# Layer 0's statistics by batch-norm instructions, a replanned order with late loads, and the last mask on TensorE, in a two-layer graph kernel

## The chip, the cores and the metric

The kernel runs on one core of a Trainium2 chip. The metric is the device time of one execution in microseconds (us), as a median of a few executions; lower is better. A core has TensorE (PE, matrix products), VectorE (DVE), ScalarE (ACT), GpSimd (POOL) and SyncE (SP, whose queue issues nearly all DMA transfers here: all but 6 of the 901 issues that the profile of the kernel before lists).

## The reference, cut to what matters

The input x is 128 batches of 128 nodes by 512 features. Layer 0 has the same adjacency for both weights, so its inner max collapses to one number per row.

```python
A = einsum('od,bdn->bon', adj, x)                 # "conv"
out0 = max_n(relu(A + b))  -> one number r per row
x = layernorm(x + r)                              # layer 0
qkv = x @ w_qkv;  8 heads
attn = softmax(where(mask == 0, -inf, q k^T * scale))
o = (attn v) @ w_proj + b_proj
x = layernorm(x + o + layernorm(o) * gamma + beta)  # layer 1
```

Adding r to a whole row does not change the row's variance and moves its mean by r. So the statistics of x + r follow from those of x, which are known as soon as x is loaded. The change uses this.

## The kernel before

Batches go in groups of four. For each group TensorE does twelve "dense" products (q, k, v; each product in three split parts), four scores, four attention products, four output projections, and the conv of a group two ahead. The kernel gives each engine its instructions in the order of one plan, a list sorted by a planned time. The planned times come from a table O of offsets from the TensorE step to which an operation belongs. An offset thus decides what stands ahead of what on each engine, and nothing else.

```python
def add_0(b):                 # ScalarE: x + r in place, with the row sum
    nc.scalar.activation(xs[b], xs[b], AF.Identity, bias=rms[g][:, i:i+1], accum_out=mv0s[g][:, i, 0:1])
def stats_0(b):               # ScalarE: sum of squares about the mean
    squares(xs[b], mv0s[g][:, i, :])
...                           # rstd_0, shift_0: five small GpSimd operations
def norm_0(b):                # ScalarE: normalize in place
    nc.scalar.activation(xs[b], xs[b], AF.Identity, bias=nm, scale=rstd)
def x_halves(b):              # ScalarE copies x into two planes of half words; SyncE stores them ("rowsx")
    planes = work.tile([P, 2, D], U16, tag="xplanes", bufs=1)
    nc.scalar.copy(planes, ...)
    nc.sync.dma_start(rows["x", b], planes)
def crossbar_x(b):            # SyncE: transposing load; xT takes a buffer of the same four as load_x
    pts[b] = xpool.tile([P, KC, P], FP, tag="xt")
    nc.sync.dma_start_transpose(pts[b]..., rows.pop(("x", b))...)
def halves(b): ...            # the same for the attention weights: ScalarE copy of 1.8 us, "planes", then "rows"
def crossbar_T(b): ...        # transposing load eT, read by the attention product
def split_d(key, gpsimd): ... # residue part x_d = x_h - x_l..., on VectorE or GpSimd by a flag 'd'
...
O = {'softmax': {'halves': [1.11, 11.24, 0.39, 2.34], 'weights': [10.99, 14.73, 21.85, 34.94], ...},
     'stats_0': [-7.16, -8.5, 6.68, -15.05], ... 'two': {'d': [1, 0, 1, 0, 0, 1, 0, 1], ...}}
```

Of the kernel before, what the change touches and what calls it, by code (L numbers as in the profile page):

```python
# [26 lines left out]
def tile_adj_resnorm_d2(  # L27
# [198 lines left out]

    def norm_0(b, vector=False):
        rstd, nm = norms.pop((b, 0))
        if vector:
            nc.vector.tensor_scalar(xs[b], xs[b], rstd, nm, op0=ALU.mult, op1=ALU.add)  # L230
            return
        nc.scalar.activation(xs[b], xs[b], AF.Identity, bias=nm, scale=rstd)  # L232
# [117 lines left out]
    def scores(b):  # L350
# [4 lines left out]
        pscs[b] = psc = ps_2.tile([P, 2, HP, P], FP, tag="ps2", name=f"psc_{b}")  # L355
        for hp in range(HP):
            for s in range(2):
# [3 lines left out]
                    start=True, stop=True,  # L361
                )

    def masked(b):
        if b < B - 1:
            e = work.tile([P, H, P], FP, tag="e", bufs=3, name=f"e_{b}")
        else:

            e = work.tile([P, 2, H * P], U16, tag="planes", bufs=1, name=f"e_{b}")
            e = e.rearrange("p s m -> p (s m)").bitcast(FP).rearrange("p (h m) -> p h m", h=H)  # L370
        nc.vector.scalar_tensor_tensor(  # L371
# [3 lines left out]
        es[b] = e  # L375

    def row_max(b):
        nmax = small.tile([P, H], FP, tag="nmax", name=f"nmax_{b}")
        nc.vector.tensor_reduce(nmax, es[b], AX.X, ALU.max, negate=True)  # L379
        es[b] = es[b], nmax  # L380

    def exps(b):
        e, nmax = es[b]
        sums = small.tile([P, H], FP, tag="sums", name=f"sums_{b}")
        for j in range(H):
            nc.scalar.activation(  # L386
                e[:, j, :], e[:, j, :], AF.Exp, bias=nmax[:, j : j + 1],
                accum_out=sums[:, j : j + 1],
            )
# [81 lines left out]
    def residual_o(b):  # L471
        engine = nc.gpsimd if b < B - G else nc.vector
# [35 lines left out]
    def norm_2(b):  # L508
# [9 lines left out]
    O = {'add_0': [-28.01, -2.67, 12.08, -40.74],  # L518
 'conv_max': [4.55, 4.72, 6.29, 4.66],
 'dense_order': [('dense', 4), ('dense', 5), ('conv', 3), ('conv', 2), ('dense', 6), ('dense', 8),  # L520
                 ('dense', 7), ('dense', 11), ('dense', 10), ('dense', 9)],
 'final': {'norm_1': [5.56, 10.5, 14.34, 13.61],
           'norm_2': [12.82, 25.73, 75.6, 26.29],
           'residual': [-18.87, -9.5, -3.43, -8.74],
           'residual_o': [5.36, 6.15, 8.98, 4.31],
           'residual_x': [-41.8, -51.69, -15.49, -25.59],
           'stats_1': [5.17, 9.89, 7.71, 8.6],
           'stats_2': [12.28, 13.13, 19.78, 20.53]},
 'last': {'norm_1': [9.58, 9.14, 7.67, 8.6],
          'norm_2': [13.12, 22.67, 13.86, 10.82],  # L530
          'residual': [-2.72, -10.61, 6.62, -30.79],
          'residual_o': [3.24, 7.11, 7.11, 5.39],
          'residual_x': [-30.28, -1.34, -16.65, -32.32],
          'stats_1': [5.84, 4.73, 7.43, 4.32],
          'stats_2': [9.71, 14.36, 12.44, 9.12]},
 'load': [0.06, -0.01, -14.55, -3.61],
 'main': [2.3, -0.65, -0.19, 0.11, 5.34, 0.19, 4.21, -1.68, -1.36, -0.44, 0.62, -1.65],
 'norm_0': [16.54, 23.0, -1.62, 2.96],
 'norm_1': {'norm_1': [15.62, 20.63, 12.47, 19.45],
            'norm_2': [19.7, 33.16, 22.1, 38.56],  # L540
            'residual': [-0.58, -15.25, 2.03, 5.96],
            'residual_o': [5.96, 9.31, 4.86, 18.97],
            'residual_x': [19.5, -11.28, 9.99, -11.76],
            'stats_1': [10.06, 13.22, 5.06, 7.83],
            'stats_2': [17.31, 22.7, 14.78, 24.32]},
 'o_d': [15.21, 7.81, 2.7, 7.93],
 'o_high': [3.47, -4.38, -3.96, 9.85],
 'o_hl': [0.41, 5.8, 1.75, 8.23],
# [3 lines left out]
 'po_main': [0.7, -1.26, 2.4, -0.02],  # L552
 'po_rest': [0.12, 0.1, 1.9, 0.12],
 'pro': {'add': [-13.57, -12.84, -10.58, -8.9],
         'conv_max': [-14.9, -13.17, -12.81, -10.03],
         'copy': [-10.01, -7.16],
         'd': [-6.26, -20.85, -4.47, -9.88],
         'gamma': [42.69],
         'high': [-19.62, -3.45, -16.17, -13.31],
         'keep': [-1.39, 0.62],  # L560
         'load': [-4.65, -6.62, 1.94, 0.39],
         'norm': [-10.64, -8.84, -7.55, -2.23],
         'relu': [-13.82, -12.91, -10.66, -9.37],
         'rstd': [-13.4, -9.99, -8.25, -3.85],
         'split': [-7.87, -6.72, -3.41, -3.99],
         'stat': [-13.43, -12.09, -8.81, -4.38],
         'w': [-7.75, -6.02, -3.34, 1.69, 4.45, 6.04, 7.57, 11.57, 13.9, 13.27, 22.03, 16.92, 41.13,
               46.85, 57.05, 54.2],
         'wrest': [-7.26, 6.82, -0.99, 3.59, -9.44, 9.43, 6.9, 4.63, 7.79, 15.59, 14.21, 1.4, 21.84,
                   31.66, 38.37, 46.51]},  # L570
 'pro_order': [('conv', 0), ('conv', 1), ('conv', 2), ('conv', 3), ('x', 0), ('x', 1), ('v', 0),
               ('x', 2), ('v', 1), ('x', 3)],
 'relu_0': [6.8, -8.71, 1.47, -7.29],
 'rest': [6.51, 1.71, 1.45, 0.9, 11.28, 4.35, 11.73, -0.79, 1.66, -0.35, 0.99, 4.88],
 'rstd_0': [16.44, -5.55, 4.82, -18.77],
 'softmax': {'cross': [-12.79, -9.61, -18.95, -6.28],
             'exps': [10.86, 9.05, 42.17, 22.92],
             'halves': [1.11, 11.24, 0.39, 2.34],
             'masked': [0.34, 3.01, 1.47, 17.35],
             'row_max': [16.52, 12.06, 18.4, 20.81],  # L580
             'weights': [10.99, 14.73, 21.85, 34.94]},
 'stats_0': [-7.16, -8.5, 6.68, -15.05],
# [254 lines left out]
```

## Time and profile before

| quantity | before |
|---|---|
| time, median of 3 (range) | 1981.43 us (1975.82 to 1982.25) |
| profiled span, mean granted clock | 1978.3 us, 0.990 |
| busy: PE, DVE, ACT, POOL | 1860.2, 1617.9, 1625.2, 1328.5 us |
| start, middle, end | 91.2, 1784.1, 102.9 us |

Start, middle and end are cut at the first instruction of the q/k product 6 of group 1 and of group 31. Inside the middle I cut each group at two more places. **d9** is the end of ScalarE's copy of the last q/k product (number 9) of a group, and places such as "d9 + 1.8" count from there. For the lengths of stretches, here and in the tables, I cut at the end of TensorE's last matmul of that product, which is 0.30 us later in the kernel before. **conv** is the start of the next group's first conv matmul. The stretch from d9 to conv holds the attention and projection, that from conv to d9 the rest. Means over groups 2 to 27 for the kernel before: d9 to conv 30.46 us, conv to d9 28.94, a whole group 59.39.

The prediction below shows the main lines of this profile. Three more are needed later. The first is from the table by stretches (columns: start and end of the stretch, its length, busy time and count of PE, PEld, DVE, ACT, POOL, then clock, DMA share and GB/s), the second from the list of VectorE's waits (total us, times, longest), the third from the list of groups of instructions (busy us, mean ns, idle ahead).

```profile
1090.55:1110.55 20.00, 19.11 (x76) 14.10 (x76) 18.47 (x30) 16.20 (x48) 17.40 (x27) 1.00 0.46 142
```

```profile
DVE qkT L348 <- ACT qkT L344: 96.9, 63, 5.5
```

```profile
L263 DVE TENSOR_TENSOR x_l<-xT,xh 128x512 fp32r<-128x512 f32 x124 | 87.7, 707 | 5.1 <-PE pm_(0, 2)_577 L310 0.7
```

The first covers the 20 us from 1 us before a conv (at 1091.55). VectorE is busy in 18.47 of them. The second says where VectorE's slack is: 96.9 us, all at the sums of q/k products, waiting for ScalarE's copies. The third is VectorE's pass that makes the low half of a split, 707 ns.

### The profile page before, as it was taken

The numbers are of one execution on the slowest core, as the hardware profiler recorded it, in microseconds if no ns is written. First come the engines' busy times: TensorE is split into PE (matmuls) and PEld (weight loads), VectorE is DVE, ScalarE is ACT, GpSimd is POOL, SyncE is SP. The second block draws the span as 40 slices with busy tenths as digits, with TensorE's granted clock in tenths as the row PEclk, the third lists the DMA queues.
The fourth block names the chain that finished last, engine by engine and source line by source line (L and its number), as shares of the span: only waits on it lengthen the run. The fifth ranks groups of instructions, "written<-read, shape, count | busy, mean of one in ns | idle before, by whom it ended". The sixth has DMA issues, their size and how long they took to land.

```text
span 1978.3 us, 33244 instructions
## 1 busy us (share of the span) xinstructions
PE 1860.2 (94%) x10537; PEld 1435.6 (73%) x10537; DVE 1617.9 (82%) x2485; ACT 1625.2 (82%) x4158; POOL 1328.5 (67%) x1970
## 2 busy tenths in 40 slices
PE   7799999999999999999999999999999999999995
PEld 4577777777777777777777777777777777777773
DVE  6788888878888888888878888877788878888885
ACT  5788888888888788888888888888888888878763
POOL 4166767766677766777766767766767766767767
PEclk9999999999999999999999999999999999999997
DMA  4465556665665665566675566665565675665541
GB/s 129 101 171 145 159 162 160 155 172 152 148 162 161 159 181 150 150 162 159 161 181 149 154 165 164 160 172 144 155 158 159 165 179 145 159 154 159 137 118 48
DMA packets 486144, 302.94 MB, mean 153 GB/s; under 512 B 399440, under 2 KB 403664, under 8 KB 485969
## 3 DMA queue, kind: packets, MB, share of 16 engines
q1 hardware_dynamic: 485104, 299.70, 58.5%
q8 instruction: 84, 1.38, 0.3%
q10 hardware_dynamic: 864, 1.12, 0.2%
q14 instruction: 92, 0.75, 0.1%
HBM read 72.16 MB, written 131.07 MB: 103 GB/s over the span
## 4 chain that ended last, share of the span: by engine, by line
PE 61%; ACT 14%; DVE 10%; DMA 8%; issue 5%; POOL 2%; SPq 0%; DVEq 0%; ACTq 0%; POOLq 0%
PE pa L186 5%; ACT e L386 4%; DMA xt<-in_x_dram 3%; DMA rowsx<-xplanes 2%; ACT xplanes L244 2%; ACT planes L401 2%; PE psc L359 2%; PE pav L432 2%; DMA eT<-rows 2%; ACT xt L232 2%; ACT square L484 1%; DVE x_l L263 1%; DVE xh L261 1%; DVE v L348 1%; DVE e L371 1%
## 5 line engine op out<-in xcount | busy, mean ns | idle before, releaser
L386 ACT ACTIVATE e<-e,nmax 128x128 f32<-128x128 f32 x1024 | 396.2, 391 | 74.1 <-DVE nmax L379 74.1
L490 POOL TENSOR_SCALAR sum<-sum 128x1 f32<-128x1 f32 (+1 forms) x322 | 102.1, 317 | 203.6 <-ACT square L484 188.4
L401 ACT COPY planes<-e 128x2048 uint16<-128x2048 uint16 x124 | 234.1, 1888 | 1.8 <-issue 1.8
L491 POOL TENSOR_TENSOR sum<-sum,mhalf 128x1 f32<-128x1 f32 (+1 forms) x322 | 212.8, 661 | 26.8
L484 ACT ACTIVATE square<-o,sum 128x512 bf16<-128x512 f32 x256 | 183.5, 717 | 24.1 <-DVE o L478 22.4
L386 ACT ACTIVATION_READ_ACCUMULATOR e<-e,nmax 128x1 f32 x1024 | 194.7, 190 | 0.0
L456 POOL TENSOR_TENSOR xb<-xb,beta_sb 128x512 f32<-128x512 f32 x128 | 176.9, 1382 | 10.7
L395 DVE TENSOR_TENSOR e<-e,sums 128x1024 f32<-128x1024 f32 x128 | 173.7, 1357 | 4.4
L432 PE MATMUL pav<-eT,v 128*64 128x128 f32 x2048 | 142.3, 282 | 32.8 <-DMA eT<-rows 18.1
L496 POOL TENSOR_SCALAR sum<-sum 128x1 f32<-128x1 f32 x256 | 100.5, 392 | 101.7 <-DVE o L478 99.1
L473 POOL TENSOR_TENSOR xb<-xb,o 128x512 f32<-128x512 f32 x124 | 161.9, 1306 | 4.8
L244 ACT COPY xplanes<-xt 128x1024 uint16<-128x1024 uint16 x124 | 129.3, 1043 | 31.6 <-DMA rowsx<-xplanes 29.6
L432 PEld LDWEIGHTS pav<-eT,v 128*64 128x64 f32 x2048 | 112.1, 138 | 59.4 <-DVE x_l L263 21.9
L379 DVE TENSOR_REDUCE nmax<-e 128x8 f32<-128x1024 f32 x128 | 154.9, 1211 | 0.0
L371 DVE SCALAR_TENSOR_TENSOR e<-psc,mask 128x1024 f32<-128x1024 f32 x128 | 152.9, 1214 | 0.7 <-PE psc L359 0.7
L186 PE MATMUL pa<-xt,adjT 128*128 128x512 f32 x256 | 123.9, 607 | 25.9 <-DMA xt<-in_x_dram 16.5
L455 POOL TENSOR_SCALAR xb<-xb,sum 128x512 f32<-128x512 f32 x128 | 127.2, 994 | 25.3 <-DMA xb<-in_x_dram 24.6
L359 PE MATMUL psc<-qkT 64*128 64x128 f32 x2048 | 142.0, 284 | 1.9 <-DVE e L371 1.9
L359 PEld LDWEIGHTS psc<-qkT 64*128 64x128 f32 x2048 | 123.4, 189 | 25.4 <-issue 23.0
L213 POOL TENSOR_SCALAR sum<-sum 128x2 f32<-128x2 f32 (+1 forms) x66 | 31.2, 472 | 161.9 <-ACT xt L202 161.6
L202 ACT ACTIVATE xt<-xt,rm 128x512 f32<-128x512 f32 x128 | 91.9, 718 | 43.8 <-POOL rm L196 43.8
L511 ACT ACTIVATE o<-o,sum 128x512 f32<-128x512 f32 x128 | 100.8, 814 | 23.9 <-POOL sum L499 23.8
(4653 smaller groups left out, 5770.0 us busy)
## 6 DMA issues: line engine op xcount, KB each, us to landing
rows<-planes SPq DMA_DIRECT2D x124, 512.0 KB, 3.3
xt<-in_x_dram SPq DMA_DIRECT2D x128, 256.0 KB, 3.5
xb<-in_x_dram SPq DMA_DIRECT2D x128, 256.0 KB, 2.9
out_dram<-o SPq DMA_DIRECT2D x128, 256.0 KB, 2.4
rowsx<-xplanes SPq DMA_DIRECT2D x124, 256.0 KB, 2.5
wraw<-in_L_gnn_w_qkv_dram SPq DMA_DIRECT2D x8, 256.0 KB, 3.2
xT<-rowsx SPq DMA_TRANSPOSE x124, 3.5
eT<-rows SPq DMA_TRANSPOSE x124, 4.8
```

Of the source, the lines that this page charges most:

```text
L186: nc.tensor.matmul(pa[b], adjT, xs[b], start=True, stop=True)
L244: nc.scalar.copy(planes, xs.pop(b).bitcast(U16).rearrange("p (m s) -> p s m", s=2))
L359: nc.tensor.matmul(psc[:, s, hp, :], qkT[hs, hp, i, :], qkT[hs, KC + hp, i, :], start=True, stop=True,)
L371: nc.vector.scalar_tensor_tensor(e, pscs.pop(b).rearrange("p s a m -> p (s a) m"), scale, mask_b, op0=ALU.mult, op1=ALU.add,)
L386: nc.scalar.activation(e[:, j, :], e[:, j, :], AF.Exp, bias=nmax[:, j : j + 1], accum_out=sums[:, j : j + 1],)
L395: nc.vector.tensor_tensor(e, e, sums[:, :, None].to_broadcast([P, H, P]), op=ALU.mult)
L401: nc.scalar.copy(planes, e.rearrange("p h m -> p (h m)").bitcast(U16).rearrange("p (m s) -> p s m", s=2),)
L432: nc.tensor.matmul(pavs[b][s * HD : (s + 1) * HD, hp, :], v[:, h * HD : (h + 1) * HD], eT[:, s * HP + hp, :], start=True, stop=True,)
L456: nc.gpsimd.tensor_tensor(xbs[b], xbs[b], beta_sb, op=ALU.add)
L473: engine.tensor_tensor(xbs[b], xbs[b], os[b], op=ALU.add)
L484: nc.scalar.activation(square, x, AF.Square, bias=s[:, 0:1], scale=-float(D), accum_out=s[:, 1:2],)
L491: nc.gpsimd.tensor_tensor(s, s, mhalf[:, :n], op=ALU.pow)
```

## The change

Its intent is to take work from ScalarE, whose backlog delays the transfers that TensorE waits for. The statistics of x for the first two batches of each group (and all four of the first group) go to VectorE's batch-norm instructions, straight from the loaded x. The whole order is planned anew, with loads landing late allowed, and the last batch's mask is added by TensorE into the scores' accumulation. A flag also moves one residue split per group from VectorE to GpSimd.

```diff
+    def stats_x(b):
+        st = small.tile([P, 6], FP, tag="bnst", bufs=2)
+        nc.vector.bn_stats(st, xs[b])
+        nc.vector.bn_aggr(mv0s[g][:, i, 0:2], st)
+    def rstd_x(b, n):  ...   # GpSimd: var + eps, power -1/2
+    def shift_x(b, n): ...   # GpSimd: r - (mean + r), times rstd
...
-    def scores(b):
+    def scores(b, with_mask=False):
+        if with_mask:        # last batch only
+            for s in range(2):
+                nc.tensor.matmul(psc[:, s], ident, mask[:, None, :].to_broadcast([P, HP, P]), start=True, stop=False)
...
-            'halves': [1.11, 11.24, 0.39, 2.34],
+            'halves': [1.39, 11.44, 0.41, 1.51],
-            'weights': [10.99, 14.73, 21.85, 34.94]},
+            'weights': [9.88, 15.04, 21.28, 31.87]},
- 'stats_0': [-7.16, -8.5, 6.68, -15.05],
+ 'stats_0': [-4.47, 4.59, 27.53, -16.8],
-         'd': [1, 0, 1, 0, 0, 1, 0, 1],
+ 'two': {'bn': [1, 0],
+         'd': [1, 1, 1, 0, 0, 1, 0, 1],
+         'tail_mask': [0, 0, 0, 1],
- 'x_cross': [-8.02, -8.17, -10.06, 4.43],
+ 'x_cross': [-8.02, -4.16, -10.12, 2.52],
...                          # some 270 more offsets, and other flags
```

## The prediction

> **What bounds the kernel now.** I read the page first. Its first part gives each engine's busy time, its second the busy tenths of TensorE over the span.
>
> ```profile
> PE 1860.2 (94%) x10537; PEld 1435.6 (73%) x10537; DVE 1617.9 (82%) x2485; ACT 1625.2 (82%) x4158; POOL 1328.5 (67%) x1970
> ...
> PE   7799999999999999999999999999999999999995
> ```
>
> TensorE is busy 94% of 1978.3 us and all but the first and the last slices show 9: it is the bound, and only its idle time, 118 us, can be won. The table by stretches (engines in the order PE, PEld, DVE, ACT, POOL; then clock, DMA share, GB/s) says where that lies.
>
> ```profile
> 0.00:20.00 20.00, 10.23 (x21) 4.89 (x22) 8.99 (x17) 10.23 (x22) 7.37 (x24) 0.87 0.47 148
> 20.00:40.00 20.00, 17.86 (x59) 10.38 (x58) 17.68 (x28) 12.61 (x23) 9.89 (x16) 0.96 0.46 137
> ...
> 1700.00:1800.00 100.00, 96.27 (x587) 75.79 (x586) 80.86 (x123) 85.93 (x223) 66.58 (x101) 1.00 0.66 164
> ...
> 1940.00:1960.00 20.00, 13.59 (x75) 10.27 (x76) 12.38 (x21) 7.64 (x13) 13.90 (x19) 0.83 0.16 53
> ```
>
> The start (0 to 100 us) leaves 25 us idle, the end (1900 to 1978) 28 us, the 1800 us between some 65 us, in crumbs: 3.7 us in a full stretch of 100. The list of TensorE's waits (total us, times, longest) names those crumbs.
>
> ```profile
> PE pav L432 <- DMA eT<-rows: 18.1, 19, 2.5
> PE pa L186 <- DMA xt<-in_x_dram: 16.5, 16, 1.8
> PE pav L432 <- DVE x_l L263: 7.3, 11, 0.8
> PE pa L186 <- DVE xh L261: 5.5, 6, 1.0
> ```
>
> Where they sit comes from TensorE's timeline, group 18 (four batches are a group; a group takes 59.0 us here, from one first conv at 1091.55 to the next at 1150.54, and 59.4 on average over the middle 28). Going through all groups, the attention product of a group's fourth batch waits 25.4 us in all (18.1 named for the transposed weights eT, 7.3 put down to VectorE, which I take for the same transfer), the first conv of the next group 25.2 us (16.6 named for the load of x), and one projection 7.7 us (a PSUM buffer that ScalarE frees). Nothing else counts.
>
> ```profile
> 1139.22 1.09 PE L432 MATMUL pav<-eT,v 128*64 128x128 f32 x16 [0.83 <-DMA eT<-rows]
> ...
> 1150.54 1.95 PE L186 MATMUL pa<-xt,adjT 128*128 128x512 f32 x4 [0.54 <-DMA xt<-in_x_dram]
> ```
>
> Both DMA waits hang on one chain. ScalarE runs without a gap from 1127 to 1143 (sequence below, each start where the one before ends), and the copy of x into half-word planes is at its end:
>
> ```profile
> 1138.21 1.89 ACT L401 COPY planes<-e 128x2048 uint16<-128x2048 uint16 x1
> 1140.00 0.72 ACT L484 ACTIVATE square<-o,sum 128x512 bf16<-128x512 f32 x1
> ...
> 1140.71 0.81 ACT L232 ACTIVATE xt<-xt,sum 128x512 f32<-128x512 f32 x1
> 1141.55 1.05 ACT L244 COPY xplanes<-xt 128x1024 uint16<-128x1024 uint16 x1
> ```
>
> SyncE's queue then takes rowsx, the transpose xT and only after it the next loads of x:
>
> ```profile
> 1142.63 0.38 SPq L246 DMA_DIRECT2D rowsx<-xplanes  x1
> 1146.08 1.23 SPq L250 DMA_TRANSPOSE xT<-rowsx  x1
> 1147.36 1.18 SPq L91 DMA_DIRECT2D xt<-in_x_dram  x2
> ```
>
> So 8.0 us after ScalarE's copy ends (1142.5) the conv starts (1150.54), 0.54 us late. eT of batch 71 likewise is issued at 1134.50, right behind a rowsx that ScalarE's earlier copy released at 1134.03, and lands 0.83 us late. ScalarE's backlog in 1120 to 1143 is what TensorE pays for twice a group.
>
> [...] xT waits for rowsx, 1142.63 to 1146.08, and the x load stands behind both. [...] The conv's max, also one pass, takes 680. [...] I estimate 0.7 us from that reduction[...].
>
> **The change part by part.** Rows concerned:
>
> ```profile
> L484 ACT ACTIVATE square<-xt,sum 128x512 bf16<-128x512 f32 x128 | 92.2, 721 | 1.0
> L202 ACT ACTIVATE xt<-xt,rm 128x512 f32<-128x512 f32 x128 | 91.9, 718 | 43.8 <-POOL rm L196 43.8
> ...
> L190 DVE TENSOR_REDUCE rm<-pa 128x1 f32<-128x512 f32 x128 | 84.5, 680 | 3.1 <-PE pa L186 3.1
> ```
>
> (1) *Statistics.* 66 batches (4 of group 0, 2 of each other group) lose an add and a square on ScalarE. In the timeline such an op keeps the engine 0.72 to 0.85 us with its accumulator read, so 132 x 0.75 = 99 us of ScalarE's 1625, 3.0 us a group. VectorE gains 66 x 0.9 = 59 us. Reordering also moves 30 of its subtractions to GpSimd (one flag per group): 30 x 1.16 = 35 us less for VectorE, 30 x 1.3 = 39 us more for GpSimd, which in turn saves about 0.7 us per pair on smaller statistics (2.4 us for six small ops now, some 1.7 for five). So ScalarE falls to about 77%, VectorE goes from 1618 to about 1642 (83 to 84%), GpSimd from 1328 to about 1340. None becomes the bound. The new VectorE ops stand at a place where VectorE now idles 2.2, 0.5, 1.0 and 1.35 us (1109 to 1121).
>
> The saved ScalarE ops stood at 1102 to 1117, before a wait for TensorE (0.97 us at 1119.5), so alone they'd be worth little.
>
> (2) *Order.* What makes them count: the half-word copy of the fourth batch's weights (1.79 us), which now stands at 1120.0 behind that wait, comes before it, into the freed time. I went through ScalarE's new list from 1120 with the trace's durations. It is the same work less 1.79 us. The first normalization waits for VectorE's second statistic and GpSimd's five small ops, to about 1121.0; then 0.7 + 0.95 (copy), 3.3 us until its rowsx lands (one plane buffer), 0.95, eight exps 3.1, 0.7, 0.95: the third copy ends at 1131.8 instead of 1133.9. Then 0.5 + 0.5 + 0.7 + 3.1 + 1.8 + 0.8 + 0.7 + 0.95: the fourth ends at 1140.7 instead of 1142.5. So eT lands some 2.1 us and x some 1.8 us earlier. The mean waits are 25.4/30 = 0.85 and 25.2/30 = 0.84 us a group; but TensorE will arrive at the conv 1.1 us earlier, so of the conv's wait perhaps 8 us stay, of eT's 4.
>
> (3) *Buffers.* The first value product of a group takes the two-bank PSUM tile and the first projection the single banks, so the second projection needs banks that VectorE frees early: 7.7 us go.
>
> (4) The middle: 65 - 8 - 4 - 7 (the rest as now) - 5 (new small waits, a guess) = 41 us won.
>
> (5) *Start.* First group: statistics need only the load, not the conv. TensorE's transposes wait 1.6 + 3.8 us now; ScalarE loses eight ops there. But x of group 1 is loaded later, behind weights, and its fourth conv may wait. I put 6 us. (6) *End.* The last mask costs two fp32 matmuls of 0.86 us, like a conv, where TensorE idles, and saves a 1.21 us VectorE pass; the exps then read PSUM. A GpSimd residual addition moves behind a split that TensorE waits for at 1941 (1.27 us). Together 3 us.
>
> Sum 41 + 6 + 3 = 50 us. Each is the best a hand replay gives, and such replays leave out collisions; I keep about four fifths: 41 us. 1981 - 41 = **1940 us**.
>
> **The rivals.** *A: the gain stays in ScalarE.* Off the bound, 99 us less ScalarE work could only lengthen its idle time, the transfers landing as late as now. For it: the removed ops lie before a wait. Against: the copy moved across that wait. Worth: start and end only, 1970. *B: a new wait replaces the old.* eT of a group's first two batches is now issued about 9 us before use instead of 13, behind a load of xb that waits for VectorE's normalization; landing takes 4.8 us by the page's issue list but up to 8.0. With 0.7 us a group lost, 1961. *C: VectorE becomes the bound of the stretch* around 1120, statistics being ahead of the last q/k sums. I count 1.8 us added against 5 us idle, so hardly; 1965. *D: all waits go.* The best groups now take 58.3 us, still with 1.2 us of waits; all at 57.2 gives 65 us, and 1912.
>
> **Range and chances.** The main path gives 1930 to 1950, A to C 1961 to 1970, each with something like one chance in eight or less, D less still. I take 1918 to 1964 for 8 in 10. The 2% line is 1941.8, right beside the middle: faster by over 2% 0.50, within 2% 0.48, slower 0.02.
>
> **What would show it right or wrong.** Right: TensorE's waits for eT and x fall from 18.1 and 16.5 us to a few each; a group takes about 58.0 us; ScalarE's busy time falls by about 100 us; VectorE's batch-norm rows show near 0.7 us; the projection's wait for v is gone. (2) is wrong if ScalarE's fourth copy still ends 1.5 us or less before the conv's former slack; (1) if the statistic takes far over 0.7 us; B shows as new waits at the first attention products. The prediction fails low if start and end shed far more than 9 us, and high if new crumbs fill the middle.

The 0.9 us a batch in step (1) is the estimate of 0.7, from the 680 ns of the conv's max, and a smaller part for the second instruction, for which it named no measurement; it enters VectorE's busy time of 1642 us alone. Two durations stand there without their source in the trace of the kernel before: the 3.3 us until a rowsx lands runs from SyncE's issue at 1123.71 to ScalarE's next copy at 1127.06, and the 0.86 us is twice the 0.43 us between the starts of a conv's two matmul records.

## The result, and the profile after

The changed kernel took **2002.16 us** (median of 4, 1996.44 to 2007.21) where the kernel before took 1981.84 beside it. Ratios in this document are the mean time of one kernel's fast runs over that of the other's fast runs of the same rounds, so not quite the ratio of the quoted medians. Here it is 1.0108, with a 95% interval of 1.0072 to 1.0145. The change made the kernel 1.1% slower. The prediction of 1940, 1918 to 1964, was wrong.

| | before | after | difference | predicted |
|---|---|---|---|---|
| start | 91.2 | 86.3 | -4.9 | -6 |
| middle | 1784.1 | 1808.7 | +24.6 | -41 |
| end | 102.9 | 99.6 | -3.3 | -3 |
| d9 to conv, mean | 30.46 | 30.62 | +0.16 | |
| conv to d9, mean | 28.94 | 29.66 | +0.72 | |
| a group, mean | 59.39 | 60.28 | +0.89 | about -1.4 |

The column "predicted" has the parts as the prediction summed them, before it kept four fifths of the sum. Start and end did what was expected. All of the miss lies in the middle. First the line of busy times on the page, then the stretches that answer to those of the prediction:

```profile
PE 1869.2 (94%) x10541; PEld 1439.7 (72%) x10541; DVE 1658.0 (83%) x2587; ACT 1543.2 (77%) x3894; POOL 1339.8 (67%) x1965
```

```profile
0.00:20.00 20.00, 11.11 (x25) 4.86 (x25) 10.74 (x23) 4.73 (x7) 7.97 (x30) 1.00 0.50 153
...
1700.00:1800.00 100.00, 96.67 (x534) 74.23 (x534) 84.44 (x131) 79.77 (x200) 71.61 (x112) 1.00 0.58 160
...
1940.00:1960.00 20.00, 14.21 (x80) 10.90 (x79) 11.82 (x22) 6.72 (x14) 18.78 (x24) 0.78 0.13 40
```

ScalarE fell by 82 us, VectorE rose by 40, GpSimd by 11. The first and the last stretch show TensorE a little busier, 11.11 and 14.21 us against 10.23 and 13.59. The full stretch of 100 us looks no better than before, so I went to TensorE's waits:

```profile
PE pa L186 <- DMA xt<-in_x_dram: 46.4, 24, 4.4
PE pav L471 <- DMA eT<-rows: 15.0, 19, 3.0
```

The wait for eT fell from 18.1 to 15.0 us, but the conv's wait for x rose from 16.5 to 46.4 us, with 24 waits of up to 4.4 us. One of these in TensorE's timeline (start, length, what, and in brackets the idle time ahead and its releaser), with the table for the stretch around it:

```profile
1166.22 3.51 PE L186 MATMUL pa<-xt,adjT 128*128 128x512 f32 x4 [2.40 <-DMA xt<-in_x_dram]
```

```profile
1166.00:1170.00 4.00, 3.77 (x6) 1.89 (x7) 3.97 (x7) 2.95 (x4) 3.92 (x5) 0.58 0.65 202
```

The first conv at 1166.22 comes 2.40 us late, and then takes 3.51 us where the prediction's line from before shows 1.95 for the same four matmul records. The granted clock over these 4 us is 0.58; from 1165.95 to 1169.36 it is 0.50, before and after that 1.00. So this long wait costs twice: for itself, and for a stretch at half clock after it. Between 150 and 1880 us the changed kernel has six such stretches, 27.3 us long together, beside six of its seven waits longer than 2.3 us; the kernel before has one, of 3.4 us. At half speed that is 12 us more lost, and TensorE's busy time did rise by 9.0 us (1.7 of it for the mask's two matmuls: four records, whose starts lie 0.43 us apart).

Per group the 0.89 us is then, from TensorE's idle gaps over groups 2 to 27: the conv's wait +0.76 (0.88 to 1.64), half clock about +0.46 (half of 0.92 us more at half clock), new waits ahead of products 4 and 6 +0.21, the waits of the attention products -0.23 (0.85 to 0.62), those of the projections -0.27. The sum is 0.93, close to the loss.

Why is the conv late? ScalarE, around the d9 ahead of that conv:

```profile
1129.37 1.90 ACT L440 COPY planes<-e 128x2048 uint16<-128x2048 uint16 x1 [1.29 <-issue]
...
1132.94 0.60 ACT L371 ACTIVATE qkT<-pm_(18, 9)_11443 128x512 f32<-128x512 f32 x1 [0.47 <-PE pm_(18, 9)_11443 L337]
1135.53 0.81 ACT L259 ACTIVATE xt<-xt,sum 128x512 f32<-128x512 f32 x1 [2.00 <-POOL sum L250]
1136.38 1.05 ACT L271 COPY xplanes<-xt 128x1024 uint16<-128x1024 uint16 x1
```

The q/k copy ends at 1133.53, that is d9. The half-word planes of the attention weights already stand ahead of it, as the prediction had it. But the first normalization starts only at 1135.53: it waits 2.00 us for GpSimd's shift (L250). Over all groups such waits of ScalarE are 60.9 us (31 waits), and the first normalization starts at d9 + 1.80 (median) where it started at d9 + 1.68 before, behind the planes. The fourth copy of x ends at d9 + 21.68 instead of 21.75, so the chain to the conv has gained nothing:

```profile
1157.56 0.58 SPq L273 DMA_DIRECT2D rowsx<-xplanes  x1
1161.17 1.23 SPq L277 DMA_TRANSPOSE xT<-rowsx  x1
1162.45 1.05 SPq L91 DMA_DIRECT2D xt<-in_x_dram  x2
```

SyncE still goes rowsx, transposed load, load of the next x. Finally the rows of the instructions concerned:

```profile
L542 DVE SCALAR_TENSOR_TENSOR o<-o,sum,gamma_sb 128x512 f32<-128x512 f32 x128 | 118.4, 925 | 92.2 <-POOL xb L512 88.2 <-POOL sum L535 4.0
...
L290 DVE TENSOR_TENSOR x_l<-xT,xh 128x512 fp32r<-128x512 f32 x124 | 115.0, 927 | 6.9 <-PE pm_(0, 3)_620 L337 1.8 <-PE pm_(0, 2)_582 L337 0.5 <-PE pm_(0, 9)_506 L337 0.5
...
L233 DVE BATCH_NORM_STATS2 bnst<-xt 128x6 f32<-128x512 f32 x66 | 45.3, 686 | 1.7 <-DMA xt<-in_x_dram 1.7
...
L234 DVE BATCH_NORM_AGGREGATE sum<-bnst 128x2 f32<-128x6 f32 x66 | 12.0, 182 | 2.3
```

The batch-norm pair costs 686 + 182 ns. VectorE's low half now takes 927 ns on the mean, where it took 707; its first normalizing pass (L542) takes 925 and waits 88.2 us for GpSimd's residual sum, where it took 790 and waited 5.0. ScalarE's statistics are down from 128 to 62. The mean of the low half hides two sizes: 30 of the 124 passes took 1.66 us (median) and 94 took 0.69. Each of the 30 began while one of GpSimd's residue subtractions (L302) was running, and none of the 94 did. In the kernel before, two passes began so, and these two were long. I come back to this at e14.

### The profile page after: what moved, and what is told of

Read it like the earlier page. It is cut to its first block, busy times and chain, and to the rows that moved or that the text cites. A ratio compares the mean times of both kernels' runs of the same rounds, so it can differ in the third digit from the quotient of the medians.

```text
span 1994.7 us, 33013 instructions
## 1 busy us (share of the span) xinstructions
PE 1869.2 (94%) x10541; PEld 1439.7 (72%) x10541; DVE 1658.0 (83%) x2587; ACT 1543.2 (77%) x3894; POOL 1339.8 (67%) x1965
## 4 chain that ended last, share of the span: by engine, by line
PE 51%; DVE 16%; ACT 10%; DMA 9%; POOL 7%; issue 5%; SPq 0%; DVEq 0%; POOLq 0%; ACTq 0%
DMA eT<-rows 4%; PE pav L471 3%; PE psc L391 3%; PE pa L186 3%; ACT e L425 3%; DMA xt<-in_x_dram 3%; DVE o L542 2%; DVE x_l L290 2%; DVE o L517 2%; ACT planes L440 2%; ACT xplanes L271 2%; DVE xh L288 2%; POOL sum L530 1%; DMA xb<-in_x_dram 1%; DVE o L503 1%
## 5 line engine op out<-in xcount | busy, mean ns | idle before, releaser
L425 ACT ACTIVATE e<-e,nmax 128x128 f32<-128x128 f32 x1016 | 393.5, 390 | 83.4 <-DVE nmax L416 83.3
L529 POOL TENSOR_SCALAR sum<-sum 128x1 f32<-128x1 f32 (+1 forms) x287 | 88.4, 308 | 218.7 <-ACT square L523 204.7
L523 ACT ACTIVATE square<-o,sum 128x512 bf16<-128x512 f32 x256 | 183.6, 717 | 43.0 <-DVE o L517 41.1
L302 POOL TENSOR_TENSOR x_d<-x_h,x_l 128x512 fp32r<-128x512 f32 x96 | 137.0, 1428 | 115.5 <-DVE x_l L290 92.0
L530 POOL TENSOR_TENSOR sum<-sum,mhalf 128x1 f32<-128x1 f32 (+1 forms) x287 | 195.9, 683 | 23.9
L495 POOL TENSOR_TENSOR xb<-xb,beta_sb 128x512 f32<-128x512 f32 x128 | 202.4, 1581 | 10.7
L542 DVE SCALAR_TENSOR_TENSOR o<-o,sum,gamma_sb 128x512 f32<-128x512 f32 x128 | 118.4, 925 | 92.2 <-POOL xb L512 88.2
L186 PE MATMUL pa<-xt,adjT 128*128 128x512 f32 x256 | 133.1, 647 | 55.7 <-DMA xt<-in_x_dram 46.4
L434 DVE TENSOR_TENSOR e<-e,sums 128x1024 f32<-128x1024 f32 x128 | 157.0, 1226 | 4.4
L494 POOL TENSOR_SCALAR xb<-xb,sum 128x512 f32<-128x512 f32 x128 | 116.3, 909 | 54.8 <-DMA xb<-in_x_dram 45.4
L259 ACT ACTIVATE xt<-xt,sum 128x512 f32<-128x512 f32 x127 | 102.4, 806 | 61.0 <-POOL sum L250 60.9
```

Of the source, the lines that this page charges most:

```text
L186: nc.tensor.matmul(pa[b], adjT, xs[b], start=True, stop=True)
L425: nc.scalar.activation(e[:, j, :], src[:, j, :], AF.Exp, bias=nmax[:, j : j + 1], scale=1.0 if src is e else scale, accum_out=sums[:, j : ...
L434: nc.vector.tensor_tensor(e, e, sums[:, :, None].to_broadcast([P, H, P]), op=ALU.mult)
L495: nc.gpsimd.tensor_tensor(xbs[b], xbs[b], beta_sb, op=ALU.add)
L523: nc.scalar.activation(square, x, AF.Square, bias=s[:, 0:1], scale=-float(D), accum_out=s[:, 1:2],)
L530: nc.gpsimd.tensor_tensor(s, s, mhalf[:, :n], op=ALU.pow)
```

## The experiments

Seventeen kernels were run, each of them correct. The table has them all; the kernel before measured 1984.9 to 1988.5 beside them (medians). The rounds ran on different chips, each beside the kernel before, so the ratios are what to compare between rounds. The last three columns are means over groups 2 to 27 of the profiled run.

| run | median us | ratio to before, 95% | d9 to conv | conv to d9 | group |
|---|---|---|---|---|---|
| before | 1981.8 | | 30.46 | 28.94 | 59.39 |
| after | 2002.2 | 1.0108, 1.0072 to 1.0145 | 30.62 | 29.66 | 60.28 |
| e1_stats_early | 1988.6 | 1.0031, 1.0004 to 1.0058 | 29.75 | 30.18 | 59.93 |
| e2_xT_early | 2052.8 | 1.0351, 1.0328 to 1.0374 | 31.91 | 29.88 | 61.79 |
| e3_old_stats | 2073.3 | 1.046, 1.043 to 1.049 | 31.60 | 31.25 | 62.85 |
| e4_stats_alone | 1983.2 | 1.0007, 0.9978 to 1.0036 | 30.43 | 28.98 | 59.41 |
| e5_hybrid | 1998.8 | 1.0053, 1.0020 to 1.0085 | 30.61 | 29.02 | 59.63 |
| e6_norm_late | 2053.4 | 1.0329, 1.0302 to 1.0356 | 31.78 | 30.14 | 61.93 |
| e7_early_norm | 2051.9 | 1.0324, 1.0290 to 1.0357 | 32.00 | 29.90 | 61.90 |
| e8_hybrid_halves | 1986.4 | 0.9994, 0.9970 to 1.0018 | 29.18 | 30.12 | 59.30 |
| e9_stats_in_gaps | 1987.2 | 1.0009, 0.9969 to 1.0048 | 30.65 | 29.06 | 59.71 |
| e10_after_gap | 1988.4 | 1.0014, 0.9983 to 1.0044 | 30.02 | 29.75 | 59.77 |
| e11_both_in_gap | **1957.1** | **0.9837**, 0.9806 to 0.9867 | 29.12 | 29.55 | 58.67 |
| e12_split_back | 1979.1 | 0.9953, 0.9923 to 0.9983 | 29.99 | 29.68 | 59.68 |
| e13_second_norm | 2000.9 | 1.0073, 1.0035 to 1.0111 | 30.60 | 29.56 | 60.16 |
| e14_split_moved | 1977.4 | 0.9951, 0.9924 to 0.9978 | 29.06 | 30.25 | 59.31 |
| e15_second_xT | 1996.1 | 1.0045, 1.0015 to 1.0074 | 29.75 | 30.29 | 60.04 |
| e16_split_only | 2008.0 | 1.0107, 1.0077 to 1.0138 | 30.85 | 29.70 | 60.56 |
| e17_od_first | 1995.7 | 1.0045, 1.0019 to 1.0071 | 29.01 | 30.86 | 59.86 |

### First round: which part of the new order

Theory A: the new statistics come too late for the first normalization. Theory B: a transposed load that now stands later on SyncE's queue is at fault.

**e1_stats_early** is the changed kernel with only

```diff
- 'stats_0': [-4.47, 4.59, 27.53, -16.8],
+ 'stats_0': [-14.0, -14.0, 27.53, -16.8],
```

> The changed kernel, with the two batch-norm statistics of a group asked of VectorE some 5 to 10 us earlier, and GpSimd's five small ops with them. Theory A (the first normalization of a group waits for those ops, 1.8 us after the last q/k copy instead of 0.5, and this eats the time won on ScalarE): the first normalization starts at 0.6 us or less, the fourth plane copy ends 1.0 to 1.5 us earlier (21.7 to about 20.5), the first conv's wait falls from 1.64 us a group to under 0.9, the time to 1955 to 1975. Theory B (SyncE's order is to blame: the second transpose xT stands behind a weights transfer): the conv's wait stays over 1.3 us and the time over 1990. Theory C (the batch-norm passes crowd VectorE): the time stays or rises.

It took 1988.6 us. The first normalization starts at d9 - 0.11, and d9 to conv falls by 0.87 us to 29.75, so the mechanism of Theory A is there. But the conv's wait is still 1.09 us a group (under 0.9 was expected), conv to d9 grows to 30.18, and more than half of the gain is gone. That was not foreseen.

**e2_xT_early**

```diff
- 'x_cross': [-8.02, -4.16, -10.12, 2.52],
+ 'x_cross': [-8.02, -8.17, -10.12, 2.52],
```

> The changed kernel, with only the second x transpose of a group back at its old place on SyncE, ahead of the first batch's weights transfer. Theory B: the fourth rowsx is issued 0.5 to 1 us earlier (22.7 to about 22), the second split no longer waits for its transpose, the conv's wait falls below 1.0 us a group and the time to 1965 to 1985. Theory A: the conv's wait stays near 1.4 us or more and the time at 1990 to 2002.

It took 2052.8 us, far worse: the offset also moves the normalization and the copy that are placed from it, and everything behind them on ScalarE is a microsecond later. So the run, with ScalarE's order changed too, does not test Theory B, which comes back as H2 in e15. The lesson: offsets of one plan are coupled.

**e3_old_stats** gives the groups the old statistics again, in the new order.

```diff
- 'two': {'bn': [1, 0],
+ 'two': {'bn': [0, 0],
```

> The new order, with the old statistics (add and square on ScalarE) in all groups but the first. Theory C (batch-norm itself costs): back to 1980 or less. Theories A and B (the order costs; the statistics only feed it): not below 1995, and rather 2000 to 2015, as ScalarE gets its 3 us a group back.

It took 2073.3 us. In the new order the old statistics cost 3.5% more. They stand there at places that the changed kernel never used (its offsets `add_0` of the first two batches are idle), so this is not the best that the new order can do with them.

**e4_stats_alone** is the reverse: the kernel before, with `stats_x`, `rstd_x` and `shift_x` in place of the old operations for the first two batches of every group but the first, and its own order.

```diff
+ if i // 2 == 0:                      # first pair of a group
+     for k in pair: at(max(min(early[k][1], limit - 1.5), pe["conv", k] + 0.1), stats_x, k)
+     ...                              # rstd_x, shift_x as in the change
+ else:
      ...                              # add_0, stats_0, rstd_0, shift_0 as before
```

> The old order and old start and end, with batch-norm statistics for the first pair of each group but the first: the statistics alone. Theories A and B: within 0.5% of the kernel before (1972 to 1990), since the ScalarE ops removed stood before a wait for TensorE. Theory C: slower by over 0.5% (over 1992).

It took 1983.2 us, ratio 1.0007. ScalarE is relieved of 2.7 us a group and nothing is gained. The statistics alone are worth nothing, as the prediction had said.

### Second round: where conv to d9 loses

In the changed kernel VectorE waits 2.75 us a group, in order, ahead of the second normalization of a group's fourth batch. Theory D blames this wait, Rival E the mutual slowing of VectorE and GpSimd.

**e5_hybrid** has the start and tail tables of the change (`pro`, `tail`, `final`, `last`, `tail_order`), all other offsets, and the flags of the groups, from the kernel before.

```diff
  changed kernel:
- O[k], two['d'], two['dense'], two['po']   # every k but the five above
+ O[k], two['d'], two['dense'], two['po']   of the kernel before;  two['bn'] = [0, 0]
```

> Start-up and tail as in the changed kernel (with the statistics instructions of the start, the mask on TensorE and the last adds on VectorE), every group in between in the order of the kernel before, with the old statistics. Theory A (the start and the tail gained 4.9 and 3.3 us, and the whole loss of 24.6 us is made by the new order of the groups): 1982 - 8 = 1974, middle 1784 as before, half clock below 0.3 us per group. Rival R1 (part of the loss comes from what the new start leaves behind in the buffers, and drifts through the groups): above 1980, period of a group over 59.7.

It took 1998.8 us. A group takes 59.63 us, near before's 59.39, so most of the loss of 0.89 is indeed made by the new order of the groups. The time of 1974 was missed: start and end, 95.6 and 109.1 us, are now worse than either kernel's: they use offsets of the common table too, so this mixture says nothing on their worth.

**e6_norm_late** is the changed kernel with

```diff
-            'norm_1': [11.97, 22.36, 12.88, 16.9],
+            'norm_1': [11.97, 22.36, 12.88, 19.6],
```

> The changed kernel with one instruction pair moved back: the second normalization of the fourth batch of a group stands on VectorE behind the two sums of q/k products that it overtook, as it did before the change. Theory D (the stretch from the convolution to the last q/k copy grew because VectorE, in order, waits 2.75 us there for GpSimd's residual sum, and the evacuations behind it come late): VectorE's wait ahead of that normalization falls below 1.5 us, the stretch from convolution to d9 goes from 29.66 to about 29.2, time 2002 to about 1990. Rival E (it grew because GpSimd and VectorE, working at the same time in the first 6 us after the convolution, slow each other: VectorE's low half 0.69 us before, 1.54 now): stretch and time stay within 4 us.

and **e7_early_norm** has this and e1's edit.

> The changed kernel with both: statistics placed earlier (as in the run e1_stats_early, 1988.6) and the normalization moved back (as in e6_norm_late). Theory D: the stretch from convolution to d9 falls from e1's 30.18 to about 29.5, time about 1975. Rival E: within 4 us of e1's time, the stretch above 30.0.

They took 2053.4 and 2051.9 us. VectorE's wait did not go, it moved: 3.44 us ahead of the sum of q/k product 7, which has nothing to do before ScalarE has copied that product. The idle time that I took for harm was time in which VectorE had nothing else to do. And with the normalization late, the residual load of the next group, which needs its buffer, blocks SyncE's queue ahead of the first eT: TensorE waits some 38 us for that in e6, under 2 in the changed kernel. Theory D is refuted. Rival E's forecast of the time fails too; whether the slowing that it names exists, e14 shows. (The low half of the fourth batch, its 0.69 and 1.54 us, takes 0.69 us in the kernel before and 1.51 in the changed one, means over groups 2 to 27.)

**e8_hybrid_halves** is e5 plus the new statistics placed early, and the planes of the fourth batch ahead:

```diff
+ 'bn': [1, 0],  'stats_0': [-14.0, -14.0, 6.68, -15.05]
-  'weights': [10.99, 14.73, 21.85, 34.94],  'halves': [1.11, 11.24, 0.39, 2.34]
+  'weights': [10.99, 14.73, 21.85, 31.87],  'halves': [1.11, 11.24, 0.39, 1.51]
```

> e5_hybrid plus the mechanism that the prediction relied on, alone: statistics instructions for the first two batches of each group, placed early, and only the weights and the half-word planes of the fourth batch moved ahead, so that ScalarE is free for the first normalization of the next group right after d9. Theory A (the mechanism is sound and only its neighbours in the new order spoil it): d9 to convolution falls from 30.46 to about 29.7 as in e1, convolution to d9 stays at 29.0, so 58.7 us per group and about 1974 - 20 = 1954. Rival R2 (moving the planes ahead always brings its own new wait, in VectorE's queue or as half clock): 1970 or more.

It took 1986.4 us: d9 to conv 29.18, 1.28 less than before, and conv to d9 30.12, 1.18 more. The same shift as in e1, in another order, and in the time Rival R2 was right. VectorE's table row and timeline show why (conv at 1093.05 here):

```profile
1092.05:1112.05 20.00, 18.23 (x69) 12.83 (x70) 19.61 (x32) 15.97 (x46) 18.58 (x28) 1.00 0.47 144
```

```profile
1109.25 0.68 DVE L233 BATCH_NORM_STATS2 bnst<-xt 128x6 f32<-128x512 f32 x1
...
1110.07 0.67 DVE L375 TENSOR_TENSOR qkT<-qkT,pd_(18, 5)_11269 128x512 f32<-128x512 f32 x1
...
1111.85 0.69 DVE L233 BATCH_NORM_STATS2 bnst<-xt 128x6 f32<-128x512 f32 x1
...
1112.67 0.66 DVE L375 TENSOR_TENSOR qkT<-qkT,pp_(18, 4)_11248 128x512 f32<-128x512 f32 x1
```

VectorE is busy in 19.61 of 20 us, from 1 us ahead of the conv: since conv comes earlier and VectorE's work does not, it has no slack left there. From 1.9 us ahead of the conv to 20 us behind it none of its instructions has an idle gap above 0.14 us on the mean over the groups. Both statistics stand in this stretch: one ahead of the sum for product 5, which runs at conv + 17.02 (+ 15.0 in the kernel before), one ahead of that for product 4. TensorE's product 8 waits 16.3 us in all for a VectorE sum, which by the turn of the four single PSUM banks is the one for product 5. Theory F: **VectorE's own queue behind the conv is the second bound**.

### Third round: the statistics' place on VectorE

**e9_stats_in_gaps** is e4 with the planes ahead, and each statistic where VectorE waited in e8.

```diff
- 'stats_0': [-7.16, -8.5, 6.68, -15.05],
+ 'stats_0': [-8.75, -3.0, 6.68, -15.05],
```

> The kernel before plus the statistics instructions in the groups and the planes of the fourth batch moved ahead (the mechanism of e8_hybrid_halves, without the new start and tail), but each statistics pair now stands where VectorE was waiting in e8_hybrid_halves (ahead of the sum of dense 7, and behind that of dense 6) instead of in its 22 us without a gap behind the convolution. Theory F (VectorE's own queue behind the convolution is the second bound, so that what d9 to convolution gains, convolution to d9 loses, and 1.7 us of statistics in it cost that much): convolution to d9 falls from 30.12 to about 29.1, d9 to convolution stays at 29.2 to 29.6, 58.3 to 58.9 us per group, time 1950 to 1970 against before's 1983. Rival G (a loop of another engine or of the DMA holds the period at 59.3 whatever VectorE does): 59.2 or more per group, time within 4 us of before's.

It took 1987.2 us. Conv to d9 is 29.06, as Theory F said, but d9 to conv is back at 30.65: the second statistic runs at conv + 24.7, and GpSimd has the shift only for a first normalization at d9 + 1.78. This is the changed kernel's fault, made again. The totals are those of Rival G, which this run can't exclude.

**e10_after_gap** is the changed kernel with both statistics just ahead of the normalization for which VectorE waits.

```diff
- 'stats_0': [-4.47, 4.59, 27.53, -16.8],
+ 'stats_0': [-9.2, -14.35, 27.53, -16.8],
```

> The changed kernel with nothing moved but its two statistics pairs, to the place just ahead of the normalization for which VectorE waits 2.75 us (in e1_stats_early one of them stood in the busy stretch ahead of it, one behind it). Theory F: convolution to d9 goes from 29.66 (30.18 in e1) to about 29.1, d9 to convolution to 29.8 as in e1, 58.9 us per group, time 2002 to about 1960, which is what the prediction had expected of the change. Rival G: 59.3 or more per group, time 1980 or more.

It took 1988.4 us, 1.4% above the expectation: first normalization at d9 - 0.11, conv to d9 0.43 better than e1, d9 to conv 0.27 worse. A group took 59.77 us, not 58.9, so Theory F missed here, and Rival G's numbers came. TensorE's waits for the load of x became shorter, at most 2.3 us instead of 4.4, and over the whole run TensorE lost 20.9 us to half clock instead of 31.4: in size, most of the 14 us gained over the changed kernel.

**e11_both_in_gap** meets both conditions in the order before: as e9, with both statistics together behind the sum for product 4.

```diff
- 'stats_0': [-7.16, -8.5, 6.68, -15.05],
+ 'stats_0': [-9.01, -12.62, 6.68, -15.05],
-   'weights': [..., 34.94], 'halves': [..., 2.34]
+   'weights': [..., 31.87], 'halves': [..., 1.51]
```

> As e9_stats_in_gaps, but both statistics pairs stand together, behind VectorE's sum of dense 4 and ahead of that of dense 8, where VectorE waits 1.39 us in e9_stats_in_gaps: early enough for the first normalization (GpSimd needs 2.8 us more and d9 is 10 us off), and behind the sum that TensorE waited for in e8_hybrid_halves. Theory F2 (both conditions at once are what the gain needs: statistics done 3 us ahead of d9, and none of them in VectorE's busy stretch behind the convolution): first normalization at -0.1, d9 to convolution 29.2 to 29.6, convolution to d9 29.0 to 29.5, 58.3 to 59.0 us per group, time 1950 to 1972 against before's 1984. Rival G (something else holds 59.3 to 59.7): 59.2 or more, time above 1978.

It took **1957.1 us, 1.6% less than the kernel before** (0.9837, 0.9806 to 0.9867), and beats both kernels. ScalarE and VectorE in its group 18 (conv at 1080.92, d9 at 1110.27):

```profile
1109.69 0.58 ACT L371 ACTIVATE qkT<-pm_(18, 9)_11443 128x512 f32<-128x512 f32 x1
1110.16 0.81 ACT L259 ACTIVATE xt<-xt,sum 128x512 f32<-128x512 f32 x1
```

```profile
1097.19 0.67 DVE L375 TENSOR_TENSOR qkT<-qkT,pd_(18, 5)_11269 128x512 f32<-128x512 f32 x1
...
1098.98 0.67 DVE L375 TENSOR_TENSOR qkT<-qkT,pp_(18, 4)_11248 128x512 f32<-128x512 f32 x1
1099.58 0.68 DVE L233 BATCH_NORM_STATS2 bnst<-xt 128x6 f32<-128x512 f32 x1
...
1100.39 0.66 DVE L233 BATCH_NORM_STATS2 bnst<-xt 128x6 f32<-128x512 f32 x1
```

(GpSimd's 2.8 us of the expectation: in the changed kernel the shift ends 1.8 to 5.8 us after the second aggregate, median 3.4.) ScalarE's normalization follows the copy of product 9 with no wait. VectorE's sum for product 5 runs at conv + 16.27, nothing waits for it any more, and the statistics fill the place where VectorE waited for ScalarE. d9 to conv keeps e8's gain, and of e8's loss in conv to d9 half is gone. Both stretches end just outside their ranges (29.12 and 29.55 us), while the time, the group and the normalization fall inside. Theory F2 is confirmed and Rival G refuted: e8, e9 and e11 differ only in where 1.7 us of VectorE's work stand (and e8 in its start and tail), and only the place that is neither too late for ScalarE nor in the way of TensorE gives the gain.

**e12_split_back** is e10 with the moved residue split back on VectorE.

```diff
-         'd': [1, 1, 1, 0, 0, 1, 0, 1],
+         'd': [1, 0, 1, 0, 0, 1, 0, 1],
```

> As e10_after_gap, but the residue split of the second batch of layer 1 (one per group), which the change moved from VectorE to GpSimd, is back on VectorE. Theory E (the move to GpSimd frees VectorE of 1.6 us and takes about as much back, since GpSimd's work then runs beside VectorE's split of the last batch: low half 1.66 us against 0.69 before): that low half falls to 0.7 to 1.0, VectorE's busy time rises by at most 20 us in all, and the time stays within 6 us of e10_after_gap's 1988. Rival (the move was a gain): 10 us or more slower than e10_after_gap.

It took 1979.1 us, 9 us below e10. The expected fall of VectorE's low half did not come (1.66 us as in e10), so Theory E is wrong in its detail. The gain points to the move as harmful, but the two intervals just touch.

### Fourth and fifth round: the split, and what is left

**e14_split_moved** puts the change's split into e11.

```diff
-         'd': [1, 0, 1, 0, 0, 1, 0, 1],
+         'd': [1, 1, 1, 0, 0, 1, 0, 1],
```

> e11_both_in_gap with the residue split of the second batch moved from VectorE to GpSimd, as the changed kernel has it. Theory E2 (the move costs by GpSimd's residue of the attention output coming later, for which TensorE already waits 9.4 us in all in e11_both_in_gap): that wait rises to 15 us or more, time 1957 to 1962 or more. Rival: VectorE's relief of 1.6 us per group outweighs it, time 1950 or less.

It took 1977.4 us, and the intervals of e11 and e14 lie far apart: the move costs some 20 us. The pass that moves takes 0.68 us on VectorE in e11 (the 1.6 us of the expectation belongs to the fourth batch's pass) and 1.65 us on GpSimd. TensorE's waits of the fourth projection for GpSimd's residue rose from 9.4 us (13 times) to 22.1 us (26 times). One of them:

```profile
1035.47 1.20 PE L344 MATMUL pd_('o', 63)_10588<-p_d,od 128*128 128x512 f32 x4 [0.94 <-POOL od L302]
```

The trace of this run shows two costs. One is a queue: GpSimd reaches that residue at conv + 3.25 instead of 2.29, and TensorE's waits for it grew by 12.7 us. The other is that VectorE was not relieved at all: its busy time rose from 1688.7 to 1708.8 us, with 31 passes fewer. The moved pass now runs on GpSimd while VectorE begins other passes, and those take longer. From e14, and then from e11:

```profile
1026.72 1.65 POOL L302 TENSOR_TENSOR x_d<-x_h,x_l 128x512 fp32r<-128x512 f32 x1 [1.78 <-DVE x_l L290]
1027.32 1.59 DVE L505 SCALAR_TENSOR_TENSOR o<-o,sum,xb 128x512 f32<-128x512 f32 x1
```

```profile
1017.72 0.75 DVE L505 SCALAR_TENSOR_TENSOR o<-o,sum,xb 128x512 f32<-128x512 f32 x1
...
1018.99 0.68 DVE L302 TENSOR_TENSOR x_d<-x_h,x_l 128x512 fp32r<-128x512 f32 x1
```

In e14, the 31 of the 128 passes L505 that began while a subtraction L302 ran on GpSimd took 1.59 us (median); the other 97 took 0.75. The order matters: over the kernels before, after, e11, e12, e14 and e17, all 97 low halves that began during such a subtraction took 1.56 to 1.68 us, and all 122 that began ahead of one that then overlapped took 0.69. How the 20 us divide between the two costs, no run separates.

**e13_second_norm** and **e15_second_xT** ask what still separates the changed order (e12, 59.68) from e11 (58.67).

```diff
 e13, against e12:
- 'x_halves': [-8.29, -11.6, -7.55, -7.22],  'stats_0': [-9.2, -14.35, ...
+ 'x_halves': [-8.29, -13.8, -7.55, -7.22],  'stats_0': [-9.2, -12.15, ...
 e15, against e13:
- 'x_cross': [-8.02, -4.16, -10.12, 2.52],  'x_halves': [-8.29, -13.8, ...
+ 'x_cross': [-8.02, -8.4, -10.12, 2.52],  'x_halves': [-8.29, -9.56, ...
```

(e13's second statistic keeps its place; its offset counts from the normalization that moved.)

> As e12_split_back, with one move on ScalarE: the normalization and the half-word planes of the second batch of layer 0 ahead of the old-style statistics of the third, as in the kernel before (second normalization at d9 + 2.4 in e11_both_in_gap, + 3.95 in e12_split_back). Theory H1 (ScalarE's order holds the convolution back): d9 to convolution from 30.0 to 29.5, time from 1979 to about 1965. Theory H2 (SyncE's order holds it: the transposed load of the second batch is issued at d9 + 18.9 against + 16.8 in e11_both_in_gap, behind the store of the next planes): no change, 1976 to 1982.

> As e13_second_norm, and the transposed load of the second batch stands ahead of the store of the next attention planes on SyncE's queue, as in the kernel before. Theory H2: its issue moves from d9 + 18.9 to about + 17, the last two transposed loads by about 1 us, d9 to convolution to 29.2 to 29.4, time about 1955 to 1962. Theory H1: as e13_second_norm, within 3 us.

e13 took 2000.9 us: the second normalization came 1.55 us earlier and the third and fourth 0.4 to 0.5 us later, and conv with them. Theory H1 is refuted, and H2's "no change" missed as well. e15 took 1996.1 us: the transposed load was issued at d9 + 16.3, the conv's wait fell to 0.27 us a group and d9 to conv to 29.75; so SyncE's order does hold the conv back (H2). But conv to d9 rose to 30.29, where TensorE waits for VectorE at products 4 and 6 (23.7 us). H2's time is refuted: the second bound takes the gain again.

**e16_split_only** is the changed kernel with only the split back.

```diff
-         'd': [1, 1, 1, 0, 0, 1, 0, 1],
+         'd': [1, 0, 1, 0, 0, 1, 0, 1],
```

> The changed kernel with the residue split of the second batch back on VectorE and nothing else. If the two faults are separate and add (e12_split_back was 9 us below e10_after_gap, e10_after_gap 14 below the changed kernel), the time is about 1991 to 1995. If the moved split is the whole fault, 1980 or less; if it does harm only once the statistics are in the right place, 2000 or more.

It took 2008.0 us, no better than the changed kernel (interval of the ratio the same). Of its three forecasts the last came true: with the statistics late, moving the split back gains nothing, and the faults do not simply add.

**e17_od_first** is e11 with the residue of the next group's first batch later on GpSimd, so that the residue that TensorE waits for comes first.

```diff
- 'x_d': [8.2, -1.25, -2.89, 1.7],
+ 'x_d': [10.9, -1.25, -2.89, 1.7],
```

> e11_both_in_gap with GpSimd's residue of the fourth attention output ahead of its residue of the next group's first batch. Theory E2 (this GpSimd queue is the rest of the second bound): TensorE's wait for it falls from 9.4 us to 2 or less, convolution to d9 from 29.55 to about 29.2, time 1957 to about 1947. Rival: the other split comes late in its turn and is waited for (a new wait of the first q/k products), 1957 or more.

It took 1995.7 us. The wait for GpSimd fell from 9.4 to 2.5 us, and d9 to conv was the best of all, 29.01. But product 4, the first q/k product of a group, now waits 45.7 us in all. The rival was right that a new wait takes the place, but it is named for VectorE's sum of the third projection (L505), not for the other split. Ahead of that sum VectorE is slowed as in e14: 30 of its passes for the upper half of x begin during a subtraction on GpSimd and take 1.52 us (median; nearly all others 0.42).

## Why the prediction was wrong, point by point

- **Statistics, step (1): right in size.** 686 + 182 ns against 0.9 us; ScalarE -82 us against -99; VectorE 1658 against 1642 (its low halves alone grew by 27 us); GpSimd 1340 as said. "Alone they'd be worth little": e4, 1.0007.
- **The place of the new operations, step (1): wrong.** "The new VectorE ops stand at a place where VectorE now idles" held for the kernel before, whose VectorE idles behind conv + 17. In the new order the two run at conv + 24.8 and + 26.8, so late that GpSimd's five small operations end only about 1.8 us behind d9. e1 and e10 against the changed kernel, and e11 against e9, move only them and have the first normalization at d9 - 0.11.
- **Order, step (2): this step failed.** It put the first normalization at 1121.0, which is d9 + 0.9; measured + 1.8. It had the fourth copy of x end 1.8 us earlier; measured 0.07. (Its third copy sums to 1131.65, not 1131.8, which changes nothing.) And it replayed ScalarE's list as gapless work: e1, with the normalization early, still brings that copy only 1.05 us forward, since a freed ScalarE then waits for others (in the changed kernel for VectorE's row maxima 83.3 us against 74.1 before, for its upper halves 72.3 against 31.3, for its sums 41.1 against 22.4).
- **The conv's wait, step (2).** "Perhaps 8 us stay"; it became some 49 us (46.4 named for the load of x). TensorE did arrive earlier (0.6 us, 1.1 was predicted), and the load did not.
- **Buffers, step (3): right.** The projection's 7.7 us are gone.
- **The middle, step (4): "5, new small waits, a guess", was far too small**, and had no term for the clock. Half clock alone takes 12 us more.
- **The moved split, step (1): mis-sized, and its overlap left out.** The 1.16 us is the mean of two sizes: in the kernel before the moved pass takes 0.68 us and the fourth batch's 1.70, so VectorE was to be relieved of 21 us, not 35. That passes of VectorE which begin during one of GpSimd's subtractions lengthen (the low half from 0.69 to 1.66 us in the changed kernel) was not counted. e14 measures the move as 20 us of time in a good order; e16 as nothing in the changed one.
- **Start and end, steps (5) and (6): right,** -4.9 and -3.3 against -6 and -3.
- **Rival C, "VectorE becomes the bound of the stretch", names the second bound that e8 and e11 show,** and was given too little. (In the changed kernel itself TensorE's new waits at products 4 and 6 are only 0.21 us a group; the late normalization and the half clock weigh more.) Its "1.8 us added against 5 us idle" compared a sum with idle time that lies behind the busy 17 us, not in them. Once conv comes earlier, that stretch has no idle time at all (e8).
- **The mechanism was sound, and mis-sized.** In e11 it wins 1.34 us in d9 to conv, about what the sum of step (2) needed, and gives 0.61 back in conv to d9: 20 us in the middle (1784.1 to 1764.2), half of the 41.

What stays open: in the changed order the same two conditions leave a group at 59.7 us. e13 and e15 show that SyncE's order and VectorE's queue both hold it, but no run here brought that order to 58.7. How much of the changed kernel's loss comes from VectorE's passes that GpSimd lengthens was not tested, nor was the cause of e17's wait for product 4; both are read from traces.

## What to carry to other kernels

When every engine runs in one planned order, free time on one engine is worth only what the next engine in the chain can do with it: find the second bound before crediting the first. New work has a window, late enough not to push what TensorE waits for and early enough for its own consumer, and its place in that window decided here between 0% and 1.6% at equal work. A long wait of TensorE cost more here than its length: in the changed kernel's middle, six of the seven waits longer than 2.3 us had 3.4 or 6.8 us at a granted clock of 0.50 behind them, and no shorter wait had. So I estimate that one wait of 4 us is worse than four of 1 us in different places. And before work is moved to another engine, look what will run beside it there: the mean duration of a group of passes can hide two sizes, as the 927 ns of the low half hid 0.69 and 1.66 us.

## What the traces show of the new instructions and of the clock

- Batch-norm instructions, in the changed kernel: 686 ns for the statistics of 128 x 512 fp32 from SBUF, 182 ns for the aggregate of one row of six (66 of each).
- Half clock: each trace records the granted clock stretch by stretch. Between 150 and 1880 us, all stretches at 0.50 of one kernel start whole multiples of 3.413 us apart (within 2 ns); in the changed kernel these are six, of 3.41 or 6.83 us, from 196.57 to 1346.86. I cut the traces into windows at these multiples. In the window ahead of four of these six TensorE was idle for 1.95 to 2.64 us, not the whole 3.413. Over the 19 kernels, all 68 windows at full clock with 1.96 us or more of idle time were followed by half clock, none of the 9404 with less than 1.79, and 20 of 38 between. So in these runs it is the idle time inside one window that counts: in the changed kernel a wait of 2.34 us in one window was followed by half clock, and in e10_after_gap one of 3.07 us, cut into 1.42 and 1.65, was not.
